# A graph attention kernel on one core: the head columns of layer 1 as four 64x64 products at the end of a step

## The chip, the cores and the metric

The kernel runs on one core of a Trainium2 chip. A core has five engines with a queue each: TensorE (PE: matrix products and transposes into PSUM; its weight loads are listed apart as PEld), VectorE (DVE), ScalarE (ACT), GpSimd (POOL) and SyncE (SP), which here only starts DMA transfers. Each engine works through its own queue in order, and engines wait for each other by semaphores. GpSimd also starts the indirect DMAs (gathers).

The metric is the time of one execution on the device, in microseconds (us); the lower, the better. Several executions are timed and the median is taken; one further execution is recorded by the profiler.

## What is computed

Two graph attention layers over one adjacency matrix, with B = 8 batches, N = 2048 nodes, 64 features, and 4 heads in the first layer. Scores are products of a node's features with its neighbours' features, masked by the graph, put through a softmax, and used to average the neighbours:

```python
def _gat_layer(h, mask, b):
    scores = jnp.einsum('...nd,...md->...nm', h, h)
    scores = jnp.where(mask, scores, NEG)
    attn = jax.nn.softmax(scores, axis=-1)
    return jnp.einsum('...nm,...md->...nd', attn, h) + b

mask = graph + jnp.eye(N, dtype=graph.dtype) > 0
h = jnp.einsum('bnc,hdc->bhnd', x, Wh)
out_h = _gat_layer(h, mask[None, None], bh[None, :, None, :])
cat = jnp.transpose(out_h, (0, 2, 1, 3)).reshape(B, N, H * D)
z = jax.nn.leaky_relu(cat, negative_slope=0.2)
h2 = jnp.einsum('bnk,dk->bnd', z, Wo)
out2 = _gat_layer(h2, mask[None], bo)
z2 = jax.nn.leaky_relu(out2, negative_slope=0.2)
```

After that come a layer norm with gamma and beta, the addition of x, and a second layer norm. The adjacency is sparse and its first nodes (the hubs) have many neighbours; the others have few.

## The kernel before

**Stages.** `gat_kernel` calls `fast_kernel`, and runs `general_kernel` only if a flag says that a limit was passed. `fast_kernel` has a beginning (about 0 to 126 us of the profile: x is turned, the hubs' rows of layer 1 are done, the lists of neighbours are begun), the steps of layer 1 (126 to 548 us), and layer 2 with the norms (the rest). The change lies in the steps of layer 1, `for i in range(-3, NG + 3)` at L1272, and in what they call.

**Tiling.** The nodes behind the 59 hubs form NS = 153 sets of 13. For each set a list of up to 128 nodes holds all neighbours of the set's members (`index`), and a gather (L912) fetches their rows from `table1` in DRAM into a tile `g` of 128 rows by 4 x 130 values. A step works on two sets (NG = 77). The eight batches are handled as Q = 4 pairs: a pair's even batch lies on partitions 0 to 63, its odd batch on partitions 64 to 127.

**Scores without h.** The scores of head h are x Wh' Wh x'. The product Wh' Wh of each head (64x64) lies twice in `gram[:, h, :]`, on the diagonal of a 128x128 matrix whose other quarters are zero. `own_rows(m)` (L920, GpSimd) copies the features of the own nodes of four sets into `xo` (128 partitions x 208 = 4 sets x 4 pairs x 13). `columns(g, cat)` (L926) multiplies them with two heads' `gram`, one 128x128 product for each head, into `cat[:, k, :208]`, and `keep_columns` (L932, ScalarE) copies both results into `y`. Two steps' calls, for heads 0 and 1 and for heads 2 and 3, fill the `y` of four sets. A float32 product with 128x128 weights shows as two instructions on TensorE, so a step has four for its columns.

**One step** issues, in the order of the text (the order on each engine's queue):

1. `scores(i + 1)` (L941, PE, 64x64 weights: four quarters of the array), `weigh` (L946, DVE: subtracts the mask).
2. `project(i - 1)` (L590, PE, 64x64) into a new `cat`, `leaky` (L577, ACT) copies it to `z` with the bias.
3. two copies `xTg<-bank` (L1291, ACT) of the turned rows of step i + 2, `lift` (L953, ACT: exp).
4. `values(i)` (L967, PE) and `invert` (L974, L975, DVE: 1/sum, and the product into `osb`).
5. the two gathers of step i + 5 (L912, POOL); every other step `own_rows` (L920, POOL); from step 30 on, every other step, twelve loads of x (L1050, SP) for table3.
6. `leak` (L582, DVE), in place on `z`.
7. up to step 9 a piece of the adjacency: its load (SP) and its conversion (L783, L788, POOL), and in some steps `make_keys` (L825, L829, PE; L814, ACT).
8. `second_maps(i - 2)` (L1001, PE, from `z`), `second_rows(i - 3)` (L1011, PE), `columns(i + 4)` (L926, PE) and `keep_columns` (L932, ACT).
9. `keep_own(i - 2)`: L1006 (DVE, PSUM to `own`) and L1007 (POOL, on to the large `own`); `keep_rows(i - 3)`: L1015 (DVE) and two stores of `rowt` to table2 (L1018, SP); every other step from 32 on `add_beta` (L1054 on DVE, L1055 a store on SP).
10. up to two jobs of `picks` (DVE: L842 MAX8 and L844, which sort out the neighbours for later sets).
11. four transposes of the first gathered tile into `bank[0]` (L571, PE), `turn_values` (L984, PE, from `osb`) with `keep_values` (L991, ACT, two copies to `otb`), and four transposes of the second tile into `bank[1]` (L571, PE).

**Buffers.** `cat` is one PSUM buffer (two banks): the next step's `project` waits until all readers of the last one are done. `bank[0]` and `bank[1]` are single too. The gathered tiles come from a ring of ten (`rowp`), five steps; a gather waits for `values` of five steps before. The `rowt` tiles are a ring of four. A load of x into `xb` waits for the landing of the store of that buffer (L1055). SP's queue is in order over all of these.

Of the kernel before, what the change touches and what calls it, by code (L numbers as in the profile page):

```python
# [30 lines left out]
F32 = mybir.dt.float32  # L31
# [15 lines left out]
SET = 13  # L47
# [314 lines left out]
def fast_kernel(ctx: ExitStack, tc: tile.TileContext, x, adj, Wh, bh, Wo, bo, gamma, beta, out, flag):  # L362
# [205 lines left out]
    def turn(tp, rows):  # L568

        for q in range(Q):  # L570
            nc.tensor.transpose(tp[:, q * P:(q + 1) * P], rows[:, q, 1:1 + P], ident)  # L571

    def leaky(cat, n, name):

        z = work.tile([P, HP, 2, n], F32, tag="z", name=name, bufs=3)
        for hp in range(HP):
            nc.scalar.activation(z[:, hp], cat[:, :, hp * n:(hp + 1) * n], AF.Identity, bias=bhp[:, hp:hp + 1], scale=1.0)  # L577
        return z

    def leak(z):  # L580
        f = z.rearrange("p q s n -> p (q s n)")
        nc.vector.scalar_tensor_tensor(f, f, SLOPE, f, OP.mult, OP.max)  # L582
# [338 lines left out]

    def columns(g, cat):

        n = quad(g // 2)[1] * Q * SET
        for k in range(2):
            nc.tensor.matmul(cat[:, k, :n], gram[:, g % 2 * 2 + k, :], held["x", g // 2][:, :n], start=True, stop=True)  # L926

# [231 lines left out]
    for e in es:  # L1159
        nc.vector.memset(e[:, 16 * M:16 * M + 64 - M], 1.0)  # L1160
    begin.close()
# [110 lines left out]
    for i in range(-3, NG + 3):  # L1272
# [25 lines left out]
        if 0 <= i + LOOK < NG and i > -3:  # L1298
            for j in range(2):
                gather(table1, 2 * (i + LOOK) + j, 1, rows_tile)  # L1300
# [4 lines left out]
        if i + 6 < NG and i % 2 == 0 and i >= -2:  # L1305
            own_rows((i + 6) // 2)
# [4 lines left out]
        if 0 <= i - 1 < NG:  # L1311
            leak(held["z", i - 1])
# [29 lines left out]
        if 2 <= i + 4 < NG + NG % 2:  # L1342
            columns(i + 4, cat)
            keep_columns(i + 4, cat)
        if 0 <= i < 8:
            keep_hub_turn(i % 4, cat)
        if 0 <= i - 2 < NG:
            keep_own(i - 2, ph)
        if 0 <= i - 3 < NG:
            keep_rows(i - 3, pr)  # L1350
        if i in hub_maps_at:
            keep_hub_maps(hub_maps_at[i], cat)
        if i in hub_rows_at:
            keep_hub_rows(hub_rows_at[i], cat)
        if i >= 53 and i % 2 and ahead_of_second:
            ahead_of_second.pop(0)()
# [5 lines left out]
        if 0 < i + 3 < NG:  # L1362
            turn(bank[0], rows[1, 2 * (i + 3)])
        if 0 <= i < NG:
            turn_values(i, op)
            keep_values(i, op)
        if 0 < i + 3 < NG:
            turn(bank[1], rows[1, 2 * (i + 3) + 1])
# [314 lines left out]
```

## Time and profile before

| | |
|---|---|
| three timed runs, us | 807.87, 810.82, 810.95 |
| median, us | 810.82 |
| the profiled execution, us | 808.08 |
| its span (first to last instruction), us | 806.3 |
| granted TensorE clock, mean | 0.974 |
| PE / DVE / ACT / POOL busy over the span, us | 725.3 / 585.6 / 528.1 / 448.4 |
| columns of layer 1 (L926, PE), instructions | 304, busy 65.7 us |

Times of the trace are microseconds from the span's start. A row of the timeline has a start, a duration, the engine, the line, the operation, the tiles out<-in, shapes, and how many instructions are merged into it; behind it, in brackets, the idle time of the engine before it and what ended that. Matmuls are pipelined, so the row of a group is longer than the time until the next group starts. A row of the busy times by stage has a stretch, its length, and busy time with the number of instructions for PE, PEld, DVE, ACT and POOL, then the granted clock, the busy share of the DMA engines, and GB/s.

### The profile page before, as it was taken

What the parts mean: (1) busy time and instruction counts of PE and PEld (TensorE: products, weight loads), DVE (VectorE), ACT (ScalarE), POOL (GpSimd) and SP (SyncE); (2) the same over time, 40 slices, a digit from 0 to 9 for tenths busy, and PEclk for the clock granted to TensorE, in tenths of its full rate; (3) what the DMA queues carried; (4) which work ended last, traced back from release to release, by engine and by line L of the source; (5) the groups of instructions that cost most, each with busy time, mean ns of one, the idle gap of its engine ahead of it and who ended that gap; (6) DMA issues with size and microseconds to landing.
All of it is one profiled execution on the core that took longest, in us unless ns stands there. A gap on an engine that the chain in (4) does not pass through costs nothing.

```text
span 806.3 us, 40511 instructions
## 1 busy us (share of the span) xinstructions
PE 725.3 (90%) x17324; PEld 614.8 (76%) x17324; DVE 585.6 (73%) x1313; ACT 528.1 (66%) x1140; POOL 448.4 (56%) x622
## 2 busy tenths in 40 slices
PE   4899999999999999999999999999999899988810
PEld 3566658887889998988898999977787688876710
DVE  2558824787888878888776777664249999988883
ACT  1454646776667766666776677754668898987852
POOL 4655337667455545556554555404777777777500
PEclk9899999999999999999999999999999999999975
DMA  6889625354333334544444444435976667776521
GB/s 143 229 234 228 231 68 163 100 168 107 91 90 91 93 92 118 139 137 138 138 137 136 139 136 135 130 109 157 304 229 174 185 171 229 220 200 187 169 53 33
DMA packets 80351, 121.57 MB, mean 151 GB/s; under 512 B 34627, under 2 KB 50839, under 8 KB 80163
## 3 DMA queue, kind: packets, MB, share of 16 engines
q0 software_dynamic: 24752, 65.67, 29.5%
q1 hardware_dynamic: 52067, 52.37, 22.1%
q8 instruction: 139, 2.28, 1.1%
q10 hardware_dynamic: 3344, 0.84, 0.6%
q14 instruction: 49, 0.40, 0.2%
HBM read 116.81 MB, written 18.25 MB: 168 GB/s over the span
## 4 chain that ended last, share of the span: by engine, by line
PE 68%; DVE 12%; DMA 8%; ACT 4%; SPq 3%; issue 3%; POOL 0%; ACTq 0%; DVEq 0%; POOLq 0%
PE s L941 10%; PE o L967 10%; PE bank L571 8%; PE cat L926 6%; DMA rows<-table,index 5%; PE o L984 4%; PE cat L1001 4%; PE cat L590 4%; PE oh L693 3%; PE sh L672 3%; PE t L571 3%; PE cat L1011 2%; SPq L1529 2%; PE bank L1411 2%; DMA out_dram<-y_s 2%
## 5 line engine op out<-in xcount | busy, mean ns | idle before, releaser
L912 POOL DMA_INDIRECT g<-table,index x154 | 162.7, 1057 | 166.4 <-PE o L967 134.4
L912 POOL DMA_INDIRECT rows<-table,index x153 | 159.5, 1042 | 52.1 <-issue 17.4
L577 ACT ACTIVATE z<-cat,bhp 128x208 f32<-128x208 f32 x154 | 58.5, 431 | 98.4 <-PE cat L590 92.4
L946 DVE TENSOR_TENSOR e<-s,mask 128x832 f32<-128x832 f32 x77 | 78.6, 1020 | 25.9 <-PE s L941 24.7
L571 PE MATMUL t<-ident,rows 128*128 128x128 f32 x612 | 85.2, 278 | 10.3 <-DMA rows<-table,index 5.0
L967 PE MATMUL o<-g,e 128*64 128x65 f32 x2464 | 91.5, 225 | 3.1 <-issue 2.7
L571 PE MATMUL bank<-ident,g 128*128 128x128 f32 x608 | 91.2, 273 | 0.4 <-DVE keysi L871 0.4
L967 PEld LDWEIGHTS o<-g,e 128*64 128x64 f32 x2464 | 79.6, 137 | 14.1 <-issue 3.9
L941 PEld LDWEIGHTS s<-y,xTg 64*64 64x64 f32 x4928 | 78.9, 134 | 12.9 <-issue 12.9
L941 PE MATMUL s<-y,xTg 64*64 64x52 f32 x4928 | 88.7, 220 | 0.0
L1565 ACT COPY xts<-t 128x512 f32<-128x512 f32 x153 | 82.0, 584 | 8.7 <-PE t L571 6.9
L571 PEld LDWEIGHTS t<-ident,rows 128*128 128x128 f32 x612 | 66.6, 141 | 22.1 <-issue 7.3
L1291 ACT COPY xTg<-bank 128x512 f32<-128x512 f32 x152 | 81.7, 598 | 0.0
L953 ACT ACTIVATE e<-e,shifts 128x832 f32<-128x832 f32 x77 | 78.5, 1020 | 2.1 <-DVE e L946 2.1
L571 PEld LDWEIGHTS bank<-ident,g 128*128 128x128 f32 x608 | 72.7, 141 | 3.5 <-DVE keysi L871 1.0
L783 POOL TENSOR_SCALAR a<-raw 117x1024 bf16<-117x1024 int32 x34 | 38.8, 1143 | 51.5 <-DMA raw<-in_adj_dram 44.4
L926 PE MATMUL cat<-xo,gram 128*128 128x208 f32 (+1 forms) x304 | 65.7, 338 | 0.5 <-ACT xTg L1146 0.4
L991 ACT COPY otb<-o 128x208 f32<-128x208 f32 x154 | 43.7, 335 | 21.6 <-ACT y L932 10.2
L975 DVE TENSOR_TENSOR osb<-o,rall 128x512 f32<-128x512 f32 x77 | 53.3, 692 | 2.7
L926 PEld LDWEIGHTS cat<-xo,gram 128*128 128x128 f32 x304 | 52.5, 201 | 1.0 <-ACT xTg L1146 0.7
L974 DVE RECIPROCAL rall<-o 64x8 f32<-64x8 f32 x154 | 31.4, 204 | 25.1 <-PE o L967 23.6
L1007 POOL COPY own<-own 128x104 f32<-128x104 f32 x77 | 30.5, 396 | 29.1 <-DVE own L1006 28.9
(205 smaller groups left out, 1472.2 us busy)
## 6 DMA issues: line engine op xcount, KB each, us to landing
raw<-in_adj_dram SPq DMA_DIRECT2D x34, 432.0 KB
xr_s<-table SPq DMA_DIRECT2D x19, 256.0 KB
table<-x SPq DMA_DIRECT2D x16, 260.0 KB
table<-rowt SPq DMA_DIRECT2D x152, 26.4 KB
out_dram<-y_s SPq DMA_DIRECT2D x152, 24.0 KB
x<-in_x_dram SPq DMA_DIRECT2D x24, 128.0 KB
table<-xb SPq DMA_DIRECT2D x11, 256.0 KB
table<-share SPq DMA_DIRECT2D x10, 256.0 KB
```

The source lines that it names most:

```text
L571: nc.tensor.transpose(tp[:, q * P:(q + 1) * P], rows[:, q, 1:1 + P], ident)
L577: nc.scalar.activation(z[:, hp], cat[:, :, hp * n:(hp + 1) * n], AF.Identity, bias=bhp[:, hp:hp + 1], scale=1.0)
L912: nc.gpsimd.indirect_dma_start(out=t.rearrange("n q c -> n (q c)"), out_offset=None, in_=table, in_offset=bass.IndirectOffsetOnAxis(ap=ind ...
L926: nc.tensor.matmul(cat[:, k, :n], gram[:, g % 2 * 2 + k, :], held["x", g // 2][:, :n], start=True, stop=True)
L941: nc.tensor.matmul(sp[half(r), p, (q * 2 + j) * M:(q * 2 + j + 1) * M], xt[half(p), j, q, half(r)], y[half(p), (j * Q + q) * M:(j * Q + q ...
L946: nc.vector.tensor_tensor(e[:, :16 * M].rearrange("p (a q n) -> p a q n", a=2, q=Q), sp[:, :, :8 * M].rearrange("p a (q n) -> p a q n", q= ...
L953: nc.scalar.activation(e[:, :16 * M], e[:, :16 * M], AF.Exp, bias=shifts[:, 0:1], scale=1.0)
L967: nc.tensor.matmul(op[half(p), j, o0:o0 + K1], e[:, c0:c0 + 64], rw[j][:, q, sums(p)], start=True, stop=True)
L975: nc.vector.tensor_tensor(osb, v[:, :, :, 1:K1], r.unsqueeze(3).to_broadcast([P, 4, 2, D]), OP.mult)
L991: nc.scalar.copy(ot.rearrange("c h (p w n) -> c p h w n", p=2, w=4)[:, p], v[:, :, p * 64:p * 64 + M].rearrange("c w (n h) -> c h w n", h=H))
L1291: nc.scalar.copy(t[:, k, :], bank[k])
L1565: nc.scalar.copy(xts[pair(s) % 4][:, s % 2, :], tp)
```

## The change

The columns are made in quarters of the array, with the 64x64 block of one head as weights: head k's block is taken from the partitions of half k. Each half of `xo` meets the block on its own partitions; for the other two of the four products, GpSimd copies the halves of `xo` crosswise into a new tile `xs` (`swap_rows`, two copies of 64 partitions x 208). Columns and their copy (`keep_columns`) move to the end of the step, and the transposes of the second gathered tile move ahead of `turn_values`. The gathers, `own_rows` and `swap_rows` move behind `keep_own` on GpSimd's queue; `leak` moves behind `keep_rows` on VectorE's. The ring of `z` goes from three to two tiles, and `xs` has two. The two calls of `columns` in the beginning stay as they are.

```diff
--- before.py
+++ after.py
@@ -572,7 +572,7 @@
 
     def leaky(cat, n, name):
 
-        z = work.tile([P, HP, 2, n], F32, tag="z", name=name, bufs=3)
+        z = work.tile([P, HP, 2, n], F32, tag="z", name=name, bufs=2)
         for hp in range(HP):
             nc.scalar.activation(z[:, hp], cat[:, :, hp * n:(hp + 1) * n], AF.Identity, bias=bhp[:, hp:hp + 1], scale=1.0)
         return z
@@ -919,11 +919,27 @@
         src = xT[:, :, BASE:].rearrange("c q (k s) -> c s q k", s=NS)[:, s0:s0 + w]
         nc.gpsimd.tensor_copy(t[:, :w * Q * SET].rearrange("c (s q k) -> c s q k", s=w, q=Q), src)
 
+    def swap_rows(m):
+
+        n = quad(m)[1] * Q * SET
+        t = held["xs", m] = work.tile([P, 2 * GM], F32, tag="xs", name=f"xs{m}", bufs=2)
+        for k in range(2):
+            nc.gpsimd.tensor_copy(t[half(k), :n], held["x", m][half(1 - k), :n])
+
     def columns(g, cat):
 
         n = quad(g // 2)[1] * Q * SET
         for k in range(2):
             nc.tensor.matmul(cat[:, k, :n], gram[:, g % 2 * 2 + k, :], held["x", g // 2][:, :n], start=True, stop=True)
+
+    def columns_by_halves(g, cat):
+
+        n = quad(g // 2)[1] * Q * SET
+        for off in range(2):
+            for k in range(2):
+                p = k ^ off
+                nc.tensor.matmul(cat[half(p), k, :n], gram[half(k), g % 2 * 2 + k, half(k)],
+                                 held["xs" if off else "x", g // 2][half(k), :n], start=True, stop=True)
 
     def keep_columns(g, cat):
         n = quad(g // 2)[1] * Q * SET
@@ -1158,6 +1174,7 @@
         hub_end(t)
     for e in es:
         nc.vector.memset(e[:, 16 * M:16 * M + 64 - M], 1.0)
+    swap_rows(1)
     begin.close()
 
     psumk = ctx.enter_context(tc.tile_pool(name="psumk", reuse_waits="tile", bufs=1, space=bass.MemoryType.PSUM))
@@ -1295,21 +1312,14 @@
             op = one(f"o{i}", "O")
             values(i, op)
             invert(i, op)
-        if 0 <= i + LOOK < NG and i > -3:
-            for j in range(2):
-                gather(table1, 2 * (i + LOOK) + j, 1, rows_tile)
         if NG - LOOK <= i < NG - 1:
             for j in range(2):
                 k = 2 * (i - NG + LOOK) + j
                 hub_block(k, rows_tile(f"gh{k}"))
-        if i + 6 < NG and i % 2 == 0 and i >= -2:
-            own_rows((i + 6) // 2)
         if i == 20:
             nc.gpsimd.memset(xbs[1], 1.0)
         if i % 2 == 0 and 0 <= (i - 30) // 2 <= NV:
             load_own((i - 30) // 2)
-        if 0 <= i - 1 < NG:
-            leak(held["z", i - 1])
         if i in (4, 8):
             leak(zh)
         if i >= 0:
@@ -1339,19 +1349,24 @@
             hub_rows(hub_rows_at[i], cat)
         if 0 <= i < 8:
             hub_turn(i // 4, i % 4, cat)
-        if 2 <= i + 4 < NG + NG % 2:
-            columns(i + 4, cat)
-            keep_columns(i + 4, cat)
         if 0 <= i < 8:
             keep_hub_turn(i % 4, cat)
         if 0 <= i - 2 < NG:
             keep_own(i - 2, ph)
+        if 0 <= i + LOOK < NG and i > -3:
+            for j in range(2):
+                gather(table1, 2 * (i + LOOK) + j, 1, rows_tile)
+        if i + 6 < NG and i % 2 == 0 and i >= -2:
+            own_rows((i + 6) // 2)
+            swap_rows((i + 6) // 2)
         if 0 <= i - 3 < NG:
             keep_rows(i - 3, pr)
         if i in hub_maps_at:
             keep_hub_maps(hub_maps_at[i], cat)
         if i in hub_rows_at:
             keep_hub_rows(hub_rows_at[i], cat)
+        if 0 <= i - 1 < NG:
+            leak(held["z", i - 1])
         if i >= 53 and i % 2 and ahead_of_second:
             ahead_of_second.pop(0)()
         if i % 2 == 0 and 0 <= (i - 32) // 2 <= NV:
@@ -1361,11 +1376,14 @@
                 some(1)
         if 0 < i + 3 < NG:
             turn(bank[0], rows[1, 2 * (i + 3)])
+        if 0 < i + 3 < NG:
+            turn(bank[1], rows[1, 2 * (i + 3) + 1])
         if 0 <= i < NG:
             turn_values(i, op)
             keep_values(i, op)
-        if 0 < i + 3 < NG:
-            turn(bank[1], rows[1, 2 * (i + 3) + 1])
+        if 2 <= i + 4 < NG + NG % 2:
+            columns_by_halves(i + 4, cat)
+            keep_columns(i + 4, cat)
         if NG - 3 <= i < NG:
             hub_step(i - NG + 3, bank[0])
     for k in range(3, 9):
```

## The prediction

> **What bounds the kernel now.** I looked first at the busy times by stage of layer 1, then at one undisturbed step of the timeline, engine by engine.
>
> ```profile
> 126.60:196.08 69.48, 67.14 (x1671) 58.43 (x1670) 49.68 (x124) 46.93 (x108) 47.79 (x78) 1.00 0.46 133
> 313.70:376.97 63.27, 62.93 (x1650) 56.41 (x1653) 56.09 (x143) 43.64 (x98) 36.33 (x43) 1.00 0.49 138
> 441.12:513.29 72.17, 72.17 (x1919) 65.55 (x1918) 54.88 (x116) 51.24 (x116) 40.58 (x50) 1.00 0.49 136
> ```
>
> TensorE is busy for 67.14 of 69.48, 62.93 of 63.27 and 72.17 of 72.17 us. VectorE is next: 89% in the second stretch, where the picks run, 76% in the last.
>
> ```profile
> 466.82 1.15 PE L941 MATMUL s<-y,xTg 64*64 64x52 f32 x64
> 467.79 0.55 PE L590 MATMUL cat<-otb,whT 64*64 64x104 f32 x16
> 468.27 1.15 PE L967 MATMUL o<-g,e 128*64 128x65 f32 x32
> 469.26 0.55 PE L1001 MATMUL cat<-z,woT 128*64 128x104 f32 x8
> 469.73 0.32 PE L1011 MATMUL cat<-ident,own 128*104 128x128 f32 x1
> 469.89 0.87 PE L926 MATMUL cat<-xo,gram 128*128 128x208 f32 x4
> 470.59 0.60 PE L571 MATMUL bank<-ident,g 128*128 128x128 f32 x4
> 471.03 0.56 PE L984 MATMUL o<-ident,osb 116*128 116x116 f32 x4
> 471.43 0.60 PE L571 MATMUL bank<-ident,g 128*128 128x128 f32 x4
> 471.96 1.15 PE L941 MATMUL s<-y,xTg 64*64 64x52 f32 x64
> ```
>
> From start to start a step takes 471.96 - 466.82 = 5.14 us, and every group follows the one before it. The columns hold TensorE for 470.59 - 469.89 = 0.70 us. That TensorE time saved is step time saved is seen near the end of the layer, where the last columns are half as wide:
>
> ```profile
> 523.29 1.15 PE L941 MATMUL s<-y,xTg 64*64 64x52 f32 x64
> ...
> 526.35 0.59 PE L926 MATMUL cat<-xo,gram 128*128 128x104 f32 x4
> ...
> 528.15 0.57 PE L941 MATMUL s<-y,xTg 64*64 64x52 f32 x24
> ```
>
> The columns' group is 0.28 us shorter (0.87 to 0.59), the step 0.28 (5.14 to 4.86).
>
> **The change on TensorE.** The four products become eight instructions of 208 columns on quarters of the array. Such a shape is in the step: `project`, sixteen of 104 columns, the same number of columns in all, holds TensorE for 468.27 - 467.79 = 0.48 us, a change of shape at its end included. That is the upper end; the lower is half of today's 0.70, if four quarters always run at once: 0.35. I take 0.37, near the lower, since scores of the same shape follow. The change of shape that stands ahead of the scores today (0.53 from the second transposes to the scores, against 0.44 from the first to the values' transposes) then stands ahead of the columns. Saving 0.33 a step, new step 4.81; ends 0.22 and 0.35.
>
> **What is late next on TensorE.** Times are moved into the step shown.
>
> ```profile
> 469.06 1.07 ACT L1291 COPY xTg<-bank 128x512 f32<-128x512 f32 x2
> 470.00 1.02 ACT L953 ACTIVATE e<-e,shifts 128x832 f32<-128x832 f32 x1
> 470.89 0.56 ACT L932 COPY y<-cat 128x416 f32<-128x416 f32 x1
> 471.67 0.57 ACT L991 COPY otb<-o 128x208 f32<-128x208 f32 x2 [0.22 <-ACT y L932]
> ```
>
> The transposes take the columns' place: `bank[0]` at 469.89, `bank[1]` at 470.33; the copies that free both end at 470.13. The values' transposes start at 470.77 instead of 471.03; `osb` (below) ends at 470.62. They end at 471.33, `otb` runs from 471.4 to 472.0, `y` behind it to 472.5. The next `project`, which needs `otb` and the single `cat`, starts at 466.82 + 4.81 + 0.97 = 472.60. So every cover holds, by 0.1 to 0.2 us; were ScalarE late by 0.4, the whole gain would be gone. I count nothing. Behind `y` on ScalarE's queue stands only the next `z`, which waits for `project` anyway; with two tiles `z` overwrites one that L1001 read a step earlier, so that edit costs nothing.
>
> **VectorE and GpSimd.**
>
> ```profile
> 469.93 0.69 DVE L975 TENSOR_TENSOR osb<-o,rall 128x512 f32<-128x512 f32 x1
> 470.54 0.58 DVE L582 SCALAR_TENSOR_TENSOR z<-z 128x416 f32<-128x416 f32 x1
> 471.55 0.27 DVE L1006 COPY own<-cat 128x104 f32<-128x104 f32 x1 [0.43 <-ACT y L932]
> ...
> 472.06 1.13 DVE L1054 TENSOR_TENSOR share<-share,bet 128x512 f32<-128x512 f32 x1
> ```
>
> ```profile
> 469.59 1.02 POOL L912 DMA_INDIRECT g<-table,index  x1 [2.45 <-PE o L967]
> 470.92 1.07 POOL L912 DMA_INDIRECT g<-table,index  x1 [0.30 <-PE cat L926]
> 471.99 0.64 POOL L920 COPY xo<-xT 128x208 f32<-128x208 f32 x1
> ```
>
> L1006 loses its wait for `y` and runs at 470.6 to 470.9, with GpSimd's L1007 after it and `leak` beside that. Two earlier steps price the meeting:
>
> ```profile
> 185.69 1.07 DVE L582 SCALAR_TENSOR_TENSOR z<-z 128x416 f32<-128x416 f32 x1
> ...
> 192.57 0.63 DVE L582 SCALAR_TENSOR_TENSOR z<-z 128x416 f32<-128x416 f32 x1
> ```
>
> ```profile
> 192.76 0.58 POOL L1007 COPY own<-own 128x104 f32<-128x104 f32 x1
> ```
>
> Beside L1007 `leak` took 0.63 us, 0.05 more than alone; the 1.07 fell beside a conversion of the adjacency. I take 0.05 from the nearest row; ends 0 and 0.49. In the steps with two picks VectorE's idle time is one wait of 0.34 us:
>
> ```profile
> 205.96 0.27 DVE L1006 COPY own<-cat 128x104 f32<-128x104 f32 x1 [0.34 <-ACT y L932]
> ```
>
> It needs 5.14 - 0.34 = 4.80 there, 4.85 with the 0.05, and 4.9 with what the small covers give back: saving 0.25 in such steps. The Trainium skill ("SBUF — State Buffer", Who interferes with whom) says that a VectorE operation with two SBUF inputs and a GpSimd one that reads SBUF exclude each other for a whole instruction. By that rule `leak` would wait for all of L1007; the row of 0.63 us does not agree, the one of 1.07 would.
>
> GpSimd then starts the gathers at 471.3 (bounds 471.2 and 471.5) instead of 469.59, and the second is issued by 471.3 + 1.02 + 0.30 + 1.07 = 473.7. The rows are wanted two steps on, by `bank[1]` at 470.33 + 9.62 = 479.95. What a landing may take is seen only in layer 2, in the chain that ended last:
>
> ```profile
> 560.15 3.41 DMA rows<-table,index
> ...
> 748.04 5.41 DMA rows<-table,index
> ```
>
> With 3.41 to 5.41 us the rows are there by 477.1 to 479.1: hidden, by 0.8 us at the least. A swap copy of 64 x 208 lies between L1007 (128 x 104) at its shortest and L920 (128 x 208, 0.64 above):
>
> ```profile
> L1007 POOL COPY own<-own x77: 263/280/1128, 147.6 to 547.8; 128x104 f32<-128x104 f32 x77
> ```
>
> So 0.26 to 0.64; I take 0.45, between them. For two steps GpSimd has 2 x (0.58 + 2.39) + 0.64 + 0.9 = 7.5 of 9.6 us, so the swaps are hidden behind nothing but GpSimd's own idle time, and their reader is two steps on. Behind L1007's wait for L1006 stand only the gathers and these copies.
>
> In the first ten steps the gathers now also stand behind the adjacency's piece, which waits for its load:
>
> ```profile
> 178.96 1.27 POOL L783 TENSOR_SCALAR a<-raw 117x1024 bf16<-117x1024 int32 x1 [4.34 <-DMA raw<-in_adj_dram]
> ```
>
> A gather 4 to 8 us later uses up the two steps' lead. Of the 13 x 0.33 = 4.3 us that TensorE saves there I count 1.5; ends -3 and 4.3.
>
> **SyncE.** With the loads of x its queue has no slack left:
>
> ```profile
> 439.42 6.91 SPq L1050 DMA_DIRECT2D share<-in_x_dram  x12
> ...
> 447.84 0.40 SPq L1055 DMA_DIRECT2D table<-xb  x1
> ...
> 451.42 5.53 SPq L1050 DMA_DIRECT2D xb<-in_x_dram  x12
> ...
> 461.04 1.14 SPq L1050 DMA_DIRECT2D share<-in_x_dram  x3
> ```
>
> Twelve loads, two stores of rows, the store of `xb`, and the wait of the next loads for its landing (447.84 to 451.42) make a ring: 12.00 us once, 9.62 the next time, where two steps take 10.28 now and would take 9.62. `add_beta` (472.06) reads loads begun some eleven us before, so lateness of a few us is absorbed, but not of one in every ring. Of the gain I take 3 us off; ends 0 and 8.6 (all of 26 steps).
>
> **The sum.** First steps 1.5; 20 steps tight on VectorE (196 to 234 and 314 to 377) x 0.25 = 5; 41 others (234 to 314 and 377 to 513) x 0.33 = 13.5, less 3 for SyncE; 0.3 for the two half-wide columns. Together 17 us. The span of 806.3 becomes 789, the profiled execution of 808.08 becomes 791. That execution lies at the low end of the runs, 2.7 under their median of 810.82, so I forecast a median of 793, by itself 785 to 800.
>
> **The rivals.**
>
> *SyncE's ring takes over.* Between 314 and 513 us the steps stay as long as now. What is left is 1.5 + 8 x 0.25 + 15 x 0.33 + 0.3 = 9 us: 801. For it: the ring's 12.00; against it: the 9.62 right behind. Chance 0.14.
>
> *VectorE takes over.* If `leak` costs the 0.49 beside L1007, the 20 tight steps need 5.3 and lose 0.15 each instead of gaining 0.25, 8 us less: 801. Chance 0.08. By the rule of the Trainium skill above ("SBUF — State Buffer") `leak` would cost the 0.28 of L1007's median, the tight steps would need 5.08 and save 0.06: 797.
>
> *Covers fail.* ScalarE's `y`, 0.1 us ahead of the next `project`, or `osb`, comes late by as much as the columns save: 807 to 813. Chance 0.07.
>
> *Gathers late, slower.* From the step's start the second gather is issued by 473.7 - 466.82 = 6.9 us and wanted 3.5 us into the step two on. With a landing of L us a step cannot be shorter than (6.9 + L - 3.5) / 2. That passes 4.81 at L = 6.2 and 5.14 at 6.9. At 7.4, 2 us over the longest shown, it gives 5.4, and 0.26 x 61 = 16 us: 827. For it: the DMA engines are half busy in these stretches and the new place brings the gathers beside the loads of x. Against it: 3.41 to 5.41. Chance 0.08.
>
> *The quarters don't run at once.* Eight passes of 0.176 (0.70 / 4) would be 1.41 instead of 0.70: 76 x 0.7 = 53 us, 864. Against it: `project`. Chance 0.03.
>
> **Chances and range.** My forecast has 0.60. The measurement tells 0.5% from no change, about 4 us: 806.8 to 814.9 is the same. Faster: 0.60, VectorE's 0.08 and 0.10 of SyncE's, 0.78; same: the rest of SyncE's and the covers, 0.11; slower 0.11. The range is 784 (saving at its upper ends) to 808; under it and over it lie some 2 in 10.
>
> **What would show it.** Right: undisturbed steps of 4.8 us; the columns in some 0.37 us of TensorE; gathers issued 1.7 us later in the step; no TensorE wait for `g`. Wrong: waits of L590 for `y`, of L984 for `osb`, of L571 for the gathers, of L1054 for its load, or L926 at 1.4 us a step.

## The result, and the profile after

The changed kernel is slower: a median of 837.54 us (830.97 to 842.65, 4 runs) against 810.88 us (807.87 to 814.43, 4 runs), a ratio of 1.031 with an interval of 1.025 to 1.037. I had forecast 793 us. The profiled execution took 840.03 us, its span is 838.2 us, 31.9 us longer than before.

First the page of the changed kernel: the shares of the chain that ended last, and one of the costly groups.

```profile
PE 44%; DMA 16%; DVE 8%; issue 5%; SPq 3%; ACT 2%; POOL 1%; DVEq 0%; POOLq 0%; ACTq 0%
...
L927 POOL COPY xs<-xo 64x208 f32<-64x208 f32 (+1 forms) x76 | 29.7, 390 | 103.6 <-DMA g<-table,index 101.3
```

The first of these lines for the kernel before:

```profile
PE 68%; DVE 12%; DMA 8%; ACT 4%; SPq 3%; issue 3%; POOL 0%; ACTq 0%; DVEq 0%; POOLq 0%
```

TensorE's share of the chain was 68% before and is 44% now, that of DMA 8% and now 16%. The exchange copies cost GpSimd 29.7 us of work (0.39 us each, where 0.45 was forecast), but 103.6 us of idle time stand ahead of them, nearly all of it ended by the landing of a gather. Next, the timeline of TensorE in the changed kernel, one step without a disturbance and the start of the next:

```profile
470.11 1.10 PE L957 MATMUL s<-y,xTg 64*64 64x52 f32 x64
471.03 0.55 PE L590 MATMUL cat<-otb,whT 64*64 64x104 f32 x16
471.51 1.15 PE L983 MATMUL o<-g,e 128*64 128x65 f32 x32
472.52 0.58 PE L1017 MATMUL cat<-z,woT 128*64 128x104 f32 x8
...
474.54 0.39 PE L941 MATMUL cat<-xo,gram 64*64 64x208 f32 x2
...
474.95 1.30 PE L957 MATMUL s<-y,xTg 64*64 64x52 f32 x61
...
476.60 1.15 PE L983 MATMUL o<-g,e 128*64 128x65 f32 x32
...
479.54 0.63 PE L571 MATMUL bank<-ident,g 128*128 128x128 f32 x4 [0.70 <-DMA g<-table,index]
```

and GpSimd in the same stretch:

```profile
467.43 1.00 POOL L912 DMA_INDIRECT g<-table,index  x1 [0.30 <-PE o L983]
468.44 0.61 POOL L920 COPY xo<-xT 128x208 f32<-128x208 f32 x1
471.70 0.77 POOL L927 COPY xs<-xo 64x208 f32<-64x208 f32 x2 [2.65 <-DMA g<-table,index]
472.54 0.27 POOL L1023 COPY own<-own 128x104 f32<-128x104 f32 x1
473.25 1.02 POOL L912 DMA_INDIRECT g<-table,index  x1 [0.45 <-issue]
474.58 1.62 POOL L912 DMA_INDIRECT g<-table,index  x1 [0.30 <-issue]
```

The first step is what I forecast: the columns hold TensorE for 474.95 - 474.54 = 0.41 us instead of 0.70, and the step lasts 4.84 us. Two things then go wrong. GpSimd stood for 2.65 us until the gathers it had just issued had landed, so the next two gathers (473.25 and 474.58) are late, and in the second step shown a transpose waits for the rows of the later one (0.70 us at 479.54). And the gather issued at 474.58 runs beside the scores: from the scores' start to the values' start TensorE needs 476.60 - 474.95 = 1.65 us, against 471.51 - 470.11 = 1.40 a step earlier.

To see where the steps lose, each was cut by the starts of TensorE's groups in three parts: scores with projection (to the first product of the values), values (to the first of the second maps), and the rest (to the next scores). The step of before that the prediction shows gives 1.45, 0.99 and 2.70. Means over all steps that start after 200 us:

| kernel | steps | scores + projection | values | rest | step |
|---|---|---|---|---|---|
| before | 63 | 1.46 | 1.08 | 2.73 | 5.27 |
| changed | 64 | 1.70 | 1.25 | 2.66 | 5.61 |
| changed, its undisturbed step | 1 | 1.40 | 1.01 | 2.43 | 4.84 |

The columns' saving is in the rest (2.43 instead of 2.70), but on the mean only 0.08 of it is left there, and the first two parts, in which the change touches no product, are 0.41 us longer.

### The profile page after: what moved, and what is told of

The parts are those of the page before. It is cut to its first block, busy times and chain, and to the rows that moved or that the text cites. A ratio compares the mean times of both kernels' runs of the same rounds, so it can differ in the third digit from the quotient of the medians.

```text
span 838.2 us, 41340 instructions
## 1 busy us (share of the span) xinstructions
PE 729.7 (87%) x17628; PEld 608.6 (73%) x17628; DVE 576.6 (69%) x1313; ACT 531.5 (63%) x1140; POOL 490.5 (59%) x698
## 4 chain that ended last, share of the span: by engine, by line
PE 44%; DMA 16%; DVE 8%; issue 5%; SPq 3%; ACT 2%; POOL 1%; DVEq 0%; POOLq 0%; ACTq 0%
PE s L957 7%; DMA g<-table,index 7%; PE o L983 6%; PE bank L571 6%; PE cat L941 4%; DMA rows<-table,index 3%; PE cat L590 3%; PE o L1000 3%; PE t L571 3%; PE cat L1017 3%; SPq L1547 2%; PE sh L1245 2%; DMA out_dram<-y_s 2%; DMA xr_s<-table 2%; PE bank L1429 2%
## 5 line engine op out<-in xcount | busy, mean ns | idle before, releaser
L912 POOL DMA_INDIRECT g<-table,index x154 | 165.9, 1077 | 48.5 <-issue 22.6
L957 PEld LDWEIGHTS s<-y,xTg 64*64 64x64 f32 x4928 | 93.7, 136 | 9.4 <-issue 4.1
L957 PE MATMUL s<-y,xTg 64*64 64x52 f32 x4928 | 95.5, 219 | 2.8 <-issue 2.3
L571 PE MATMUL bank<-ident,g 128*128 128x128 f32 x608 | 82.4, 276 | 11.0 <-DMA g<-table,index 10.6
L927 POOL COPY xs<-xo 64x208 f32<-64x208 f32 (+1 forms) x76 | 29.7, 390 | 103.6 <-DMA g<-table,index 101.3
L1007 ACT COPY otb<-o 128x208 f32<-128x208 f32 x154 | 43.6, 335 | 61.6 <-PE o L1000 51.1
L571 PEld LDWEIGHTS bank<-ident,g 128*128 128x128 f32 x608 | 69.5, 142 | 14.1 <-issue 12.1
L1023 POOL COPY own<-own 128x104 f32<-128x104 f32 x77 | 37.7, 490 | 37.0 <-DVE own L1022 34.8
L1017 PE MATMUL cat<-z,woT 128*64 128x104 f32 x616 | 45.7, 267 | 6.3 <-ACT z L577 2.6
```

Of the source, the lines that this page charges most:

```text
L912: nc.gpsimd.indirect_dma_start(out=t.rearrange("n q c -> n (q c)"), out_offset=None, in_=table, in_offset=bass.IndirectOffsetOnAxis(ap=ind ...
L957: nc.tensor.matmul(sp[half(r), p, (q * 2 + j) * M:(q * 2 + j + 1) * M], xt[half(p), j, q, half(r)], y[half(p), (j * Q + q) * M:(j * Q + q ...
L1007: nc.scalar.copy(ot.rearrange("c h (p w n) -> c p h w n", p=2, w=4)[:, p], v[:, :, p * 64:p * 64 + M].rearrange("c w (n h) -> c h w n", h=H))
L1017: nc.tensor.matmul(dst, woT[:, hp, :], src, start=(hp == 0), stop=(hp == HP - 1))
```

## The experiments

Four theories. **A:** the exchange's wait for the gathers' landing holds GpSimd, and the next gathers come late. **B:** at their new place the gathers land too late by themselves. **C:** the quarters, or `leak` at its new place, cost it. **D** (formed after the first four runs): while GpSimd issues a gather, TensorE's short products, 64 in the scores and 16 in the projection, come slower, and so do its signals to other engines; the old place put the issue beside transposes, the new one beside scores and projection.

The runs fell on two kinds of chips. On the first kind the kernel before takes 811 to 813 us, on the second 942 to 956 us. Each ratio below is to the kernel before on the same chip. The changed kernel itself ran on the first kind only.

**1. The gathers' move alone.** The kernel before with this edit:

```diff
-        if 0 <= i + LOOK < NG and i > -3:
-            for j in range(2):
-                gather(table1, 2 * (i + LOOK) + j, 1, rows_tile)
...
-        if i + 6 < NG and i % 2 == 0 and i >= -2:
-            own_rows((i + 6) // 2)
...
             keep_own(i - 2, ph)
+        if 0 <= i + LOOK < NG and i > -3:
+            for j in range(2):
+                gather(table1, 2 * (i + LOOK) + j, 1, rows_tile)
+        if i + 6 < NG and i % 2 == 0 and i >= -2:
+            own_rows((i + 6) // 2)
```

> The kernel before with only the gathers and the copy of the rows moved behind the copy of the own maps; no exchange, columns and leak as before. Theory A: no new wait, so 805-816 us, the same. Theory B: steps of 5.4 us or more, 822-840 us. Theory C: the same as before, 805-816 us.

Measured on the second kind: 1.183 (1.175 to 1.191). A second time, beside the changed kernel as it is:

> The kernel before with only the gathers and the copy of the rows moved behind the copy of the own maps, a second time. Theory A: nothing waits newly for a landing, so within 0.5% of the kernel before. Theory D: the issue stands beside the scores and the projection in every step; at the stretch of the first chip (0.3 us of scores, 0.3 of projection) some 0.5 us a step, 1.03 to 1.06 times the kernel before; on a chip like that of the runs above 1.15 to 1.2.

> The changed kernel as it is, on the chip of the runs beside it, as their measure. On the chip of the first result it took 1.031 times the kernel before; on the chip of the runs above, where a gather's issue beside the scores stretched them from 1.15 us to 2-3.8 us, I expect 1.05 to 1.2; on a chip like the first 1.025 to 1.037. Theory A: GpSimd's wait of the exchange for the gathers' landing makes most of it. Theory D (new: while GpSimd issues a gather, TensorE's short products, 64 of the scores and 16 of the projection, come slower; the new place puts the issue beside them, the old one beside transposes): the scores' groups with an issue beside them take 1.4 us or more, those without one 1.15.

Measured on the first kind: the move alone 1.032 (1.024 to 1.040), the changed kernel 1.020 (1.013 to 1.028). The move by itself, with neither exchange nor quarters, costs as much as the whole change. Rows of the move alone on the first kind, from the timeline, GpSimd, ScalarE and TensorE mixed:

```profile
507.68 1.15 PE L941 MATMUL s<-y,xTg 64*64 64x52 f32 x64
...
508.37 1.02 POOL L912 DMA_INDIRECT g<-table,index  x1 [0.51 <-issue]
...
508.65 0.88 PE L590 MATMUL cat<-otb,whT 64*64 64x104 f32 x16
...
509.46 1.15 PE L967 MATMUL o<-g,e 128*64 128x65 f32 x32
...
509.91 0.76 ACT L577 ACTIVATE z<-cat,bhp 128x208 f32<-128x208 f32 x2 [1.96 <-PE cat L590]
...
510.72 0.38 PEld L1001 LDWEIGHTS cat<-z,woT 128*64 128x64 f32 x8 [0.25 <-ACT z L577]
```

and the same copy to `z` in the kernel before:

```profile
468.41 0.76 ACT L577 ACTIVATE z<-cat,bhp 128x208 f32<-128x208 f32 x2 [1.31 <-PE cat L590]
```

The projection beside the issue holds TensorE for 509.46 - 508.65 = 0.81 us (0.48 before), and ScalarE starts 0.38 us after the projection's end (508.65 + 0.88), where before it was 0.07 (467.79 + 0.55). The second maps then wait for `z`. The three parts, over the 64 steps that start after 200 us, are 1.65, 1.37 and 2.72: 0.19 and 0.28 more than before in the two parts beside the issue, and nothing in the rest. The granted clock was 1.00 from 200 to 500 us in both profiles, so the clock does not explain it. The stretch also goes with the issue inside one profile: in the kernel before, the projection takes 0.48 us in 62 of the 63 steps and 0.81 us in the one where an issue lies beside it (its rows stand in the section on why the prediction was wrong); in the run of experiment 4 it takes 0.48 us on the mean in the 43 steps without an issue beside it, and 0.71 in the 15 with more than 0.2 us of one. Rows that land late would show in the rest, where the gathered rows are transposed; in this run that wait comes to 1.7 us in all:

```profile
L571 PE MATMUL bank<-ident,g 128*128 128x128 f32 x608 | 91.1, 273 | 1.7 <-DMA g<-table,index 1.7
```

So B falls, and D stands. On the second kind the same kernel shows it larger. Its timeline:

```profile
502.59 1.00 POOL L912 DMA_INDIRECT g<-table,index  x1 [0.30 <-issue]
503.31 0.42 PE L590 MATMUL cat<-otb,whT 64*64 64x104 f32 x5 [0.34 <-issue]
...
504.04 0.42 PE L590 MATMUL cat<-otb,whT 64*64 64x104 f32 x4 [0.30 <-issue]
```

TensorE does four or five products, stands for 0.3 us though it waits for nothing that the profile shows, and goes on; scores and projection take 3.59 us of a step there, and TensorE again waits for no rows.

**2. One gather of the two moved**, the first at the old place:

> The kernel before with the second gather of each step moved behind the copy of the own maps, the first at its old place, the copy of the rows too. In the run with both moved the first issue stands beside scores and projection, the second beside the values. Theory D: the one moved issue stands beside scores and projection as the first did there, so most of the loss comes: 1.015 to 1.035. If the loss comes of the delay of the rows or of both issues alike: half of 1.032 or less, 1.00 to 1.016.

Second kind: 1.054 (1.050 to 1.058). The sizes expected were the first kind's; on another chip of this kind both cost 0.183, so one costs under a third. One late issue meets scores and projection (2.43 us); two, one behind the other, cost more than twice one.

**3. Other GpSimd work at that place.** The kernel before with

```diff
             keep_own(i - 2, ph)
+            for _ in range(3):
+                nc.gpsimd.memset(probe, 1.0)
```

> The kernel before with three GpSimd memsets of 128 x 256 (some 0.3 us each, about as long as one gather's issue) in every step behind the copy of the own maps, where the change puts the gathers; the gathers stay at their old place. If any GpSimd work beside the scores and the projection slows TensorE: projection 0.65 us or more and 1.01 to 1.03 times the kernel before. Theory D (it is the issue of an indirect DMA): projection 0.48 to 0.52 and within 0.5% of the kernel before.

Second kind: 1.005 (1.001 to 1.009), where on the same chip one gather at this place costs 0.054. So it is the gather, not GpSimd's being busy. The projection takes 0.56 us, a little over the expected 0.48 to 0.52; in the kernels of experiment 8 that have the gathers at their old place and no memsets, on this kind too, it takes 0.54. The scores, up to the projection, take 1.25 us here and 0.97 in the kernel before on the first kind: on the second kind the issues seem to reach them already from the old place.

Whether it is the issue itself or the first of the transfers that it sets going is not separated. In the kernel before, a gather's first packets come some 0.4 us after its issue begins (median), and in the rows of experiment 8 TensorE stands until 504.79 us, 0.35 us beyond the issue's end. The transfers as a whole are not it on the first kind: in the kernel before, the projection runs while the packets of the two gathers just issued are moving, and still takes 0.48 us.

**4. The wait alone.** The kernel before, gathers at their old place, with one element of each upper partition copied behind the copy of the rows:

```diff
             own_rows((i + 6) // 2)
+            nc.gpsimd.tensor_copy(probe[half(1), :], xT[half(1), 0, BASE:BASE + 1])
```

> The kernel before with one more GpSimd copy every second step, of one element in each of the partitions 64 to 127 of the turned x into a tile that nothing reads, behind the copy of the rows; in the program this copy waits for the landing of every gather issued so far, as the exchange does. The gathers stay at their old place. Theory A: the wait holds GpSimd for the landing, but the gathers of the next step start only 2.8 us into it, so they are late by 0-2 us every second step: 1.00 to 1.02 times the kernel before, with 30-80 us of idle time ahead of the copy. Theory D: late gathers fall beside the scores in every second step: 1.01 to 1.03. If the wait costs nothing, its part in the slowdown is through the place alone.

First kind: 1.012 (1.007 to 1.017). Its group:

```profile
L1308 POOL COPY probe<-xT 64x1 f32<-64x1 f32 x37 | 7.9, 214 | 95.3 <-DMA g<-table,index 95.3
```

A copy of 64 single elements gets the whole wait, 95.3 us, so neither the data nor its amount makes it. What does is seen in the semaphores that the traces list: a GpSimd copy that reads from partition 64 waits for the landing of the four gathers issued since the last such copy. GpSimd's copy that reads from partition 0 (experiment 8) waits for none, nor does the copy from partition 64 on VectorE (experiment 7) or ScalarE (experiment 8). Why the program puts the wait in was not found. It costs little where the gathers stand at their old place: the next gathers are late every second step, and the parts are 1.53, 1.13 and 2.75.

**5. Exchange ahead of the gathers**, at the new place:

```diff
+        if i + 6 < NG and i % 2 == 0 and i >= -2:
+            own_rows((i + 6) // 2)
+            swap_rows((i + 6) // 2)
         if 0 <= i + LOOK < NG and i > -3:
             for j in range(2):
                 gather(table1, 2 * (i + LOOK) + j, 1, rows_tile)
-        if i + 6 < NG and i % 2 == 0 and i >= -2:
-            own_rows((i + 6) // 2)
-            swap_rows((i + 6) // 2)
```

> The changed kernel with the copy of the rows and the two exchange copies ahead of the two gathers of their step instead of behind them; everything else as changed. Theory A (the wait of the first exchange copy for the landing of the gathers just issued stalls GpSimd's queue, and the next gathers come late): the copy now waits only for gathers that are a step old, GpSimd's idle time ahead of the exchange falls from 101 us to under 25, even steps come down from 5.5-6 us to 4.9, and the time to 785-800 us. Theory B (the gathers are too late at their new place by themselves): they are later still by some 1.5 us every second step, 835 us or more. Theory C (the columns on quarters, or leak at its new place, cost what was lost): 830 us or more.

**6. Gathers at the old place**, the exchange at the step's end:

> The changed kernel with the two gathers of a step back at their place behind the values; the copies of rows and the exchange stay at the step's end. Theory A: the exchange still waits for the gathers of its own step, but these are issued 1.7 us earlier, so the wait ends that much earlier and the next gathers are just in time: 795-812 us, with 40-80 us of GpSimd's idle time still ahead of the exchange. Theory B: the place was the fault, 785-797 us. Theory C: 830 us or more.

Second kind, same chip: 1.140 (1.131 to 1.150) and 1.044 (1.036 to 1.053). In the first of them the wait is gone, as A said, and yet it is 14% slower than before:

```profile
L927 POOL COPY xs<-xo 64x208 f32<-64x208 f32 (+1 forms) x76 | 27.4, 360 | 5.9 <-DMA g<-table,index 1.5
```

In the second the wait is kept, with the gathers at the old place:

```profile
L927 POOL COPY xs<-xo 64x208 f32<-64x208 f32 (+1 forms) x76 | 31.8, 418 | 69.6 <-DMA g<-table,index 53.0 <-issue 14.1
```

It is far better. On this kind the place outweighs the wait; A as the sole cause falls.

**7. Two ways to do without the wait that I got wrong.** The copy of the upper half given to VectorE, directly behind GpSimd's copy of the rows:

```diff
-        for k in range(2):
-            nc.gpsimd.tensor_copy(t[half(k), :n], held["x", m][half(1 - k), :n])
+        nc.gpsimd.tensor_copy(t[half(1), :n], held["x", m][half(0), :n])
+        nc.vector.tensor_copy(t[half(0), :n], held["x", m][half(1), :n])
```

with the gathers at the new place, and then at the old:

> The changed kernel with the exchange split: the lower half is copied to the upper one by GpSimd (a copy that reads from partition 0), the upper half to the lower one by VectorE; places as changed, so the gathers still stand ahead. Neither copy waits for a gather in the program. Theory A: no GpSimd idle time behind the gathers, 785-800 us (VectorE's copy of 64 x 208 every second step adds some 0.2-0.3 us where VectorE is tight: up to 3 us in all). Theory B: 830 us or more. Theory C: 830 us or more.

> The changed kernel with the gathers back at their place behind the values and the exchange split between GpSimd (lower half to upper) and VectorE (upper to lower), so that no copy waits for a landing and no issue stands beside the scores, but for the last 0.2 us of the second. Theories A and D together: the columns' saving comes out, 0.97 to 0.985 times the kernel before (785-799 us on a chip like the first). Theory C (the columns on quarters or leak's new place): slower than before. On a chip where the stretch is large, the 0.2 us of overlap may take 0.2-0.4 us of each step, and then 0.98 to 1.02.

1.284 (1.277 to 1.290) on the second kind, 1.117 (1.106 to 1.129) on the first. The group that shows why, from the run with the gathers at the new place:

```profile
L927 DVE COPY xs<-xo 64x208 f32<-64x208 f32 (+1 forms) x38 | 10.0, 266 | 140.4 <-POOL xo L920 140.3
```

VectorE works in order and now stands 140 us (74 us in the other run) for a copy that GpSimd makes behind its gathers; `rowt` behind it, and the columns that need its buffer, come late. I had moved the wait from one engine to another. These two tell nothing on C.

**8. The exchange mended.** Gathers and copy of the rows at the old place, lower half to upper by GpSimd right behind, upper half to lower by ScalarE one step later, behind `y`:

```diff
+    def swap_down(m):
+        n = quad(m)[1] * Q * SET
+        nc.scalar.copy(held["xs", m][half(0), :n], held["x", m][half(1), :n])
...
             keep_columns(i + 4, cat)
+        if i % 2 and i + 5 < NG and i >= -1:
+            swap_down((i + 5) // 2)
```

> The changed kernel with the gathers and the copy of the rows at their old place behind the values, the lower half copied to the upper by GpSimd behind the copy of the rows, and the upper half to the lower by ScalarE one step later, behind y. No copy waits for a landing, no engine waits for a copy just issued, and the gathers' issue is beside transposes. Theory A+D: the saving of the columns on quarters comes out: 0.965 to 0.985 times the kernel before, steps of 4.8 to 4.9 us. Theory C (the quarters or leak's new place cost it): 1.00 or more.

The same exchange with the gathers at the new place:

> The same exchange (up by GpSimd, down by ScalarE a step later), but the gathers at the change's place behind the copy of the own maps. Theory D (issue beside the scores and the projection): what the columns save is given back, 0.99 to 1.01 times the kernel before, scores' or projection's groups stretched in every step. Theory A (the landing wait is all): as the kernel with the old place, 0.965 to 0.985.

Second kind: 1.011 (1.007 to 1.015) and 1.149 (1.144 to 1.153). The place costs 0.138 with no landing wait in the kernel, and TensorE waits for no rows; scores and projection take 3.66 us of a step instead of 2.23. That is D alone. Both were run again for a chip of the first kind, the mended one three times, and all fell on the second:

> The mended exchange with the gathers at their old place, a second time. Theory A+D: on a chip where a moved gather costs 3% (as where the changed kernel took 1.02 to 1.03 times the kernel before) 0.965 to 0.985; on one where it costs 18%, the end of the second issue, which now falls on the scores because the step is shorter, takes most of the saving, 1.00 to 1.02 as in the first run. Theory C: 1.00 or more on either.

> The mended exchange (no wait for a landing) with the gathers at the change's place, a second time. Theory D with A: the place costs what it cost alone (1.032 on a chip like the first), the columns save 0.03, together 0.995 to 1.01, and the rest of the changed kernel's loss is the landing wait. Theory D without A: as the changed kernel, 1.02 to 1.03. Theory A alone: 0.965 to 0.985.

> The mended exchange with the gathers at their old place, a third time, for a chip like the first, where the kernel before takes some 811 us. Theory A+D: there 0.965 to 0.985 times the kernel before. Theory C: 1.00 or more. On a chip where the kernel before takes some 955 us: 1.01 as in the two runs before.

> The mended exchange with the gathers at their old place, a fourth time, again for a chip like the first. Theory A+D: 0.965 to 0.985 times the kernel before where that takes some 811 us, 1.01 to 1.02 where it takes some 950. Theory C: 1.00 or more on both.

1.013 (1.010 to 1.016), 1.152 (1.149 to 1.156), 1.017 (1.009 to 1.025) and 1.013 (1.007 to 1.020). So on this kind even the mended kernel is 1 to 2% slower than before. The timeline of its first run shows what is left:

```profile
502.99 1.45 POOL L912 DMA_INDIRECT g<-table,index  x1 [0.30 <-issue]
...
503.75 0.52 PE L960 MATMUL s<-y,xTg 64*64 64x52 f32 x24
...
504.79 0.86 PE L960 MATMUL s<-y,xTg 64*64 64x52 f32 x40 [0.53 <-issue]
```

The step is shorter, so the second issue's end now falls on the scores: the issue takes 1.45 us instead of 1.0, and TensorE stands for 0.53 us in the middle of them. The steps, expected at 4.8 to 4.9 us, take 5.79. Is it the quarters, then, or the order? The mended kernel with the columns as four products on the whole array again:

> The mended exchange with the gathers at their old place, but the columns as four products on the whole array again, at the step's end; the exchange is still copied, and nothing reads it. Against the mended kernel (1.01 to 1.02 times the kernel before where that takes some 950 us) it tells what the quarters bring. If the quarters save what I forecast and nothing takes it back: 1.03 to 1.05 there, steps 0.33 us longer. If the shorter step gives it back, because the end of the second issue then falls on the scores (Theory D): 1.00 to 1.015 there, with the scores' groups at 1.0 to 1.2 us instead of 1.9. On a chip like the first: 0.995 to 1.01, the new order alone.

1.013 (1.008 to 1.017), the same as with the quarters. The parts, means over the steps that start after 200 us (64 and 65), the quarters from the first mended run:

| kernel | scores + projection | values | rest | step |
|---|---|---|---|---|
| mended, whole array | 1.91 | 1.05 | 2.75 | 5.71 |
| mended, quarters | 2.23 | 1.11 | 2.45 | 5.79 |

The quarters save 0.30 us in the rest, near the 0.33 forecast, and scores and projection give 0.32 back. The scores did not come back to the expected 1.0 to 1.2 us with the whole array: up to the projection they take 1.37, and 1.68 with the quarters. C falls as far as the quarters go: their saving is real, and by the rows above the issue takes it. That the order of `leak` and columns costs the 1% isn't excluded.

**9. The last overlap taken away.** In `values` the loop over the two gathers' rows is put outside that over the quarters, so that the first buffer is free half a group earlier:

> The same, and the values' products ordered by set (all of the first gather's rows, then all of the second's) instead of by quarter, so that the first row buffer is free half a group (some 0.5 us) earlier and both gathers are issued before the scores begin. Theory D: no issue falls on the scores; the scores' groups are back at 1.15 us in nearly all steps, and the time is 0.965 to 0.98 times the kernel before on either kind of chip. If the stretch of the scores is not the issue's: as the run without the new order.

Second kind: 1.026 (1.021 to 1.030), where the mended kernel beside it had 1.013. Half of D's forecast holds: scores and projection are back at 1.46 us. But the rest grew from 2.45 to 3.31. Its timeline:

```profile
507.73 1.00 POOL L912 DMA_INDIRECT g<-table,index  x1 [0.30 <-issue]
...
508.22 0.62 PE L1003 MATMUL o<-ident,osb 116*128 116x116 f32 x4
...
509.45 0.27 DVE L1025 COPY own<-cat 128x104 f32<-128x104 f32 x1 [1.29 <-PE o L1003]
509.52 0.57 ACT L1010 COPY otb<-o 128x208 f32<-128x208 f32 x2 [1.28 <-PE o L1003]
```

Those four transposes end at 508.84, and VectorE and ScalarE start 0.6 to 0.7 us later, both together. It is the usual case here: where `otb` waits for the transposes (50 steps between 200 and 520 us) it starts some 0.58 us after their end (median), in the kernel before 0.08 (14 steps). I read it by D: the issue delays TensorE's signals too, and moved off the scores it meets the transposes that `otb` waits for. No run tests this reading by itself. No version faster than the kernel before was found.

## Why the prediction was wrong

1. **What bounds the kernel, and the columns' price: right.** TensorE sets the step; the columns went from 0.70 to 0.41 us (forecast 0.37, ends 0.35 and 0.48) and the undisturbed step is 4.84 us (forecast 4.81). The saving was measured by itself in the mended kernels, 0.30 us.
2. **Covers: right for the most part.** TensorE's weight loads waited for `osb` 3.8 us in the whole layer, and 4.1 us for `z`, a cover that the prediction did not list; no wait of the projection for `y` shows in the changed kernel.
3. **`leak` beside L1007 (L1023 in the changed kernel): small, but the price fell on the other engine.** The mean of `leak` went from 591 to 619 ns, 0.03 us where 0.05 was forecast.

```profile
L582 DVE SCALAR_TENSOR_TENSOR z<-z 128x416 f32<-128x416 f32 x77 | 47.7, 619 | 0.0
```

   The two meet in 25 of the 77 steps. There `leak` takes its 0.58 us in 24, and it is GpSimd's copy that is longer: 0.91 us on the mean, 0.29 in the other 52 steps. That fits the exclusion behind the rival of 797 us, but with GpSimd as the one that is held. One such meeting:

```profile
320.55 0.77 POOL L1023 COPY own<-own 128x104 f32<-128x104 f32 x1 [1.41 <-DVE own L1022]
...
320.59 0.58 DVE L582 SCALAR_TENSOR_TENSOR z<-z 128x416 f32<-128x416 f32 x1
```

4. **The gathers' move: the step that failed.** I moved the issue from "469.59" to "471.3" in the step and asked only when the rows would be there ("hidden, by 0.8 us at the least"). That part was right: alone, the move makes TensorE wait 1.7 us for rows in the whole layer. What I did not price is the issue itself, some 2 us of each step that went from beside transposes to beside scores and projection. Moved alone it costs 1.032 (1.024 to 1.040) on the kind of chip that I predicted for, 26 us of 813, more than the 17 us that I expected to gain. In the profile before, nearly every issue lies beside wide products. But among the 63 steps after 200 us there is one where it came late and fell beside the projection:

```profile
397.44 1.15 PE L941 MATMUL s<-y,xTg 64*64 64x52 f32 x64
...
398.20 1.02 POOL L912 DMA_INDIRECT g<-table,index  x1 [2.10 <-issue]
...
398.41 0.88 PE L590 MATMUL cat<-otb,whT 64*64 64x104 f32 x16
...
399.22 1.15 PE L967 MATMUL o<-g,e 128*64 128x65 f32 x32
```

   The projection holds TensorE for 399.22 - 398.41 = 0.81 us instead of 0.48, the same 0.81 as in the moved kernel. This row could have priced the move before any run: 0.33 us a step, as much as the columns were to save.
5. **The swap copies: a second miss in the same step.** "Behind L1007's wait for L1006 stand only the gathers and these copies": the copies' 0.39 us was near (0.45 forecast, 0.26 to 0.64), but their own wait was not asked for. It held GpSimd for 101 us. At the old place such a wait costs 1.012 (1.007 to 1.017). In the changed kernel its share is open: it makes rows late, 10.6 us of TensorE's waits in the list below, but it also shifts the issues of every second step. The steps there alternate between 5.21 and 6.00 us on the mean (scores and projection 1.53 and 1.86, values 1.21 and 1.29, rest 2.46 and 2.85). If the rest's difference is put to late rows, these cost 0.20 us of the mean step, an estimate, against 0.41 in the two parts beside the issues. The changed kernel has the move's loss, the wait's, and the columns' gain at once, and the mended kernel with late gathers, which would have told the wait's share, never ran on the first kind.

```profile
POOL xs L927 <- DMA g<-table,index: 101.3, 37, 5.2
...
PEld bank L571 <- issue: 12.1, 11, 3.7
PE bank L571 <- DMA g<-table,index: 10.6, 9, 3.5
```

6. **The first ten steps: wrong by 8.7 us.** By the starts of the scores, the stretch that the prediction shows as 126.60 to 196.08 took 76.7 us instead of 69.5, where I counted a gain of 1.5. Here the landing wait is longest (5.15 us, and conversions of the adjacency stand behind it). With the move alone the same stretch took 73.6 us, with the wait alone 71.2.

```profile
184.25 0.77 POOL L927 COPY xs<-xo 64x208 f32<-64x208 f32 x2 [5.15 <-DMA g<-table,index]
185.11 1.08 POOL L783 TENSOR_SCALAR a<-raw 117x1024 bf16<-117x1024 int32 x1
```

7. **SyncE's ring:** not reached. The steps never became short enough on the mean to test it.

The rival "gathers late, slower" named 827 us and a chance of 0.08. Its sign came true, its mechanism (a long landing that the steps cannot hide) only in part, and through a wait that it did not contain; that its time lies near the measured one is luck.

## What to carry to other kernels

When an instruction is moved to another place, ask not only whether its result is still in time but what it then runs beside, and search the trace of before for the odd step where the two already meet: here an issue whose old place was beside wide products cost 3 to 18% beside short ones. A copy added on an engine that also issues transfers may come with waits of its own; look for them, or put the copy where such waits are long satisfied, and see that the engine which takes it over isn't made to wait in turn. A saving of TensorE time can come out in full at its place (0.30 us) and be lost in the next group because the step's shortening moved an overlap.

## What the runs showed of the hardware

- While GpSimd issues an indirect DMA (1.0 us), short products on TensorE come slower and signals from TensorE later: on the first kind of chip the projection took 0.81 instead of 0.48 us and `z` started 0.38 instead of 0.07 us after it; on the second, scores and projection took 3.59 us of a step. Whether the issue or the first packets that follow it do this was not separated. The issue suffers too: 1.45 and 1.62 us instead of 1.0. Three memsets at the same place cost 0.5%. The Trainium skill ("SBUF — State Buffer", SBUF: two separate sides) states that a DMA cannot be slowed by a compute operation, nor the other way round, and, of the engines' ports, that TensorE never waits on anyone. Here TensorE is slowed beside the issue of a gather (0.81 instead of 0.48 us); so as it stands the sentence does not fit; whether the two meet at SBUF's ports or elsewhere was not found.
- Two kinds of chips differ by 16 to 18% on the same kernel (811 to 813 and 942 to 956 us), and the price of the same move by a factor of six (0.032 and 0.183). Much of the first difference may have the same source: the profile of the kernel with memsets (1.005 of the kernel before) on the second kind is 152 us longer than that of the kernel before on the first, 26 us of it in the steps of layer 1 and 120 behind them, where layer 2 issues 153 more gathers; the idle time of TensorE for which the profile shows no wait is 55.7 us in it, and 2.9 on the first kind. Why the chips differ was not found.
